# Relational graph convolution with its weight products in [3,2] by [2,3] blocks

## The chip, the cores and the metric

The kernel runs on one core of one Trainium2 chip. The metric is the device time of one execution in microseconds (us). A core has TensorE (PE; its weight loads are listed apart, as PEld), VectorE (DVE), ScalarE (ACT), GpSimd (POOL) and SyncE (SP), which issues most of the transfers. Each works through its own queue in order, and semaphores hold an instruction until what it needs is there. Everything is float32.

## What is computed

A graph of 384 nodes with 12,672 typed edges passes through an attention layer and then a relational graph network. The change is in the latter's two convolution layers:

```python
def _rgcn_conv(x, src, dst, edge_type, basis, comp, root, bias):
    n = x.shape[0]
    W = jnp.einsum('rb,bio->rio', comp, basis)
    h_all = jnp.einsum('ni,rio->rno', x, W)
    counts = jnp.zeros((R, n), x.dtype).at[edge_type, dst].add(1.0)
    norm = 1.0 / counts[edge_type, dst]
    msg = h_all[edge_type, src] * norm[:, None]
    agg = jax.ops.segment_sum(msg, dst, num_segments=n)
    return agg + x @ root + bias
...
x = jax.nn.relu(h_text @ w_in + b_in)
for l in range(L):
    h_in = x
    x = _rgcn_conv(x, src, dst, edge_type, basis[l], comp[l], root[l], conv_bias[l])
    x = jax.nn.relu(x)
    x = x + h_in
    x = _batchnorm(x, bn_gamma[l], bn_beta[l])
h_final = x @ w_out + b_out
```

Here R = 6 relations, four bases for each of L = 2 layers, and 768 features. The kernel never forms W. It computes H_b = x @ basis_b for the four bases, and for each basis a mixed adjacency matrix At_b, the sum over relations of comp[r, b] times the counts A_r, divided by the number of edges of relation r that end in each node. The aggregate is then the sum over b of At_b^T H_b, a product over 4 × 384 = 1,536 rows.

## The kernel before

The first part, up to about 371 us of the span, is the attention layer, the input projection (`ps_x`) and, beside them, the tables of edge counts: GpSimd scatters counts into a table in memory (`atab`), which is read back into `A` as six matrices of 384x384 (lines 850 to 854) and summed over sources by GpSimd (`add_up`, lines 355 and 356). This part is not changed but for the first weight loads.

Then, for each layer:

- **Bases.** Node features lie transposed: `XT` has six tiles of 128 features by 384 nodes. For each basis, H has three blocks of 128 nodes by 768 outputs. The first two node blocks, two halves of the input features and two halves of the outputs form a [2,2] by [2,2] block product that is done in seven products with sums (`node_sums`, `weight_sums`, `last_sums`, all on VectorE). The third node block is done plainly in four. That is 11 products of 3 matmuls, each 128x128 weights by 384 columns: 33 matmuls a basis. The 18 plain ones (line 985, the loop over `c`) come first and the sums are made beside them. The last product of a basis (`rest`) is done within the next one. Results go from PSUM to `H_` by copies on ScalarE (lines 991 to 1006) and additions on VectorE (992, 1000, 1002).
- **Divisors and mixes**, in layer 0, put between the products by the table `between`. `share(r)` (lines 358 to 369) sums A_r's counts over all partitions with a matmul by ones, turns zero counts into one on ScalarE (364, 365), takes a reciprocal on VectorE (366) and multiplies A_r by it (367). `mix` forms At from A: on ScalarE for r = 0 (346) and on VectorE for the other five relations, one instruction of 128x1152 for each of four bases (348). Layer 1 mixes A again with its own coefficients, beside its bases.
- **Root.** x @ root, transposed, in 36 matmuls of 384 columns (line 1019) that stay in six PSUM banks `pr`; the aggregate is partly added there.
- **Aggregate.** Seven products for each pair of output tiles (`ps_c`, line 1077) with the sums `T1` to `T4` of At and `feature_sums` of H on VectorE; then `take` adds to `XN`, `rectify`, `measure` and `normalise_layer` do ReLU, the residual and the batch normalisation of each feature tile. `XN` becomes the next layer's `XT`.

Weights come through `wpool`, five buffers of up to 8 KB a partition, in thirds of a basis. TensorE, VectorE, GpSimd, SyncE and (from the second projection on) ScalarE run in the order in which the program writes the instructions. PSUM has eight banks, handed out by `next_bank` in the order of last use.

Of the kernel before, what the change touches and what calls it, by code (L numbers as in the profile page):

```python
# [10 lines left out]
F32 = mybir.dt.float32  # L11
# [6 lines left out]
P = 128  # L18
N = 384
# [9 lines left out]
HC = DC // 2  # L29
# [15 lines left out]

BQ, BK, BV, BIQ, BIK, BIV, B_IN, CB, GAM, BET, NCOL = 0, 8, 16, 24, 32, 40, 48, 54, 66, 78, 90
# [5 lines left out]
def gnn_kernel(ctx: ExitStack, tc: tile.TileContext, out, x, edges, chunks, cols, rows, small,  # L52
               wq, wk, wv, wiq, wik, wiv, wo, w_in, basis, root, w_out):
# [297 lines left out]
    taken = []  # L351
# [5 lines left out]

    def share(r):

        ps = next_bank("ps_cnt", [i for i in range(8) if i not in taken])  # L360
        nc.tensor.matmul(ps[:, :N], ones, sums[r], start=True, stop=True)
        rn = late.tile([P, N], F32, tag="rn", name="rn", bufs=2)

        nc.scalar.activation(rn, ps[:, :N], AF.Relu, bias=minus)
        nc.scalar.activation(rn, rn, AF.Identity, bias=ones[:, 0:1])
        nc.vector.reciprocal(rn, rn)
        nc.vector.tensor_tensor(A[:, r], A[:, r], rn[:, None, :].to_broadcast([P, NT, N]), ALU.mult)
        if r + 4 < R:
            add_up(r + 4)


    with ExitStack() as inner:
# [358 lines left out]
        for g in range(STEPS + 1):  # L731
            f = g + LEAD
            if g < STEPS:
                turn_probs(g)
            if f < STEPS:
                exponents(f)
            if f - 1 in total:
                normalise(f - 1)
            if f + 1 < STEPS:
                scores(f + 1)  # L740
            if g == STEPS:
                ps_y = next_bank("ps_y", (0,))
                multiply_o(ps_y, 2, 0, range(KD - 1))
            if g > 0:
                gather(g - 1)
            if f + 2 == STEPS:

                w_x = [act_tile("w_x") for _ in range(2)]
                for half in range(2):
                    load_rows(w_x[half], w_in[half])  # L750
                w_first = [wload(basis[0, 0, part], (2, DC), "w_c") for part in range(3)]
                w_first += [wload(basis[0, 1, part], (2, DC), "w_c") for part in range(2)]
# [153 lines left out]
    with tc.tile_pool(name="conv", bufs=1) as cp:  # L906

        def block(X, n, i):

            return X.rearrange("p (c i) n -> p i c n", i=2)[:, i, :, n * P:(n + 1) * P]

        def node_sums(X):
            S = cp.tile([P, 4, 3, P], F32, tag="S", name="S")
            for i, a, b, op in ((0, block(X, 1, 0), block(X, 1, 1), ALU.add), (1, S[:, 0], block(X, 0, 0), ALU.subtract),
                                (2, block(X, 0, 0), block(X, 1, 0), ALU.subtract),
                                (3, block(X, 0, 1), S[:, 1], ALU.subtract)):
                nc.vector.tensor_tensor(S[:, i], a, b, op)  # L920
            return S

        def weight_sums(w):
            T13 = keep.tile([P, 3, 2, HC], F32, tag="hT", name="T13")
            T2 = keep.tile([P, 3, HC], F32, tag="mask8", name="T2")
            for c in range(3):
                nc.vector.tensor_tensor(T13[:, c], w[c][:, :, HC:], w[c][:, 0, :].rearrange("p (o d) -> p o d", o=2),
                                        ALU.subtract)
                nc.vector.tensor_tensor(T2[:, c], w[c][:, 1, HC:], T13[:, c, 0], ALU.subtract)
            return T13[:, :, 0], T2, T13[:, :, 1]  # L930

        def last_sums(w, T2):
            T4 = cp.tile([P, 3, HC], F32, tag="T4", name="T4")
            for c in range(3):
                nc.vector.tensor_tensor(T4[:, c], w[c][:, 1, :HC], T2[:, c], ALU.subtract)
            return T4

        w_first = [w_first[:3], w_first[3:]]

        def load_basis(l, b):  # L940
            w = w_first.pop(0) if w_first else []
            return w + [wload(basis[l, b, part], (2, DC), "w_c") for part in range(len(w), 3)]


        def shares(*rs):
            return lambda: [share(r) for r in rs]

        def mixes(l, r, *bs):
            return lambda: mix(l, r, At, bs)

        between = {(0, 2, 0): shares(0), (0, 2, 1): shares(1),
                   (0, 2, 2): shares(2), (0, 2, 4): lambda: [share(3), mix(0, 0, At)],
                   (0, 3, 0): shares(4), (0, 3, 1): shares(5),
                   (0, 3, 4): lambda: [mix(0, r, At) for r in range(1, R)],
                   (1, 0, 0): mixes(1, 0, 0, 1, 2, 3)}
        for i in range(10):
            between[1, (i + 1) // 3, (i + 1) % 3] = mixes(1, 1 + i // 2, *((0, 1), (2, 3))[i % 2])

        def go_between(*site):
            between.pop(site, lambda: None)()  # L960

        S = node_sums(XT)
        w = load_basis(0, 0)
        T = weight_sums(w)
        for l in range(L):

            H_ = cp.tile([P, B, NT, DC], F32, tag="H", name="H")
            rest = lambda: None
            for b in range(B):
                hs = [[H_[:, b, n, i * HC:(i + 1) * HC] for i in range(2)] for n in range(NT)]  # L970
                pe, pf, pb, pc, pa = [next_bank("ps_g", [i for i in range(8) if i not in taken[-1:]])[:, :N]
                                      for _ in range(5)]
                taken[:] = ring[-5:]
                kept = ring[-2:]

                def times(ps, x, y, start=False):

                    for c in range(3):
                        nc.tensor.matmul(ps, x[:, c], y(c), start=start and c == 0, stop=(c == 2),  # L979
                                         skip_group_check=not start)  # L980

                for c in range(3):
                    for ps, n, i, o, first in ((pa, 0, 0, 0, True), (pe, 2, 0, 0, True), (pf, 2, 0, 1, True),
                                               (pb, 0, 1, 0, True), (pe, 2, 1, 0, False), (pf, 2, 1, 1, False)):
                        nc.tensor.matmul(ps, block(XT, n, i)[:, c], w[c][:, i, o * HC:(o + 1) * HC],  # L985
                                         start=(first and c == 0), stop=(c == 2 and (i == 1 or ps is pa)))
                    if c == 0:
                        rest()
                        T4 = last_sums(w, T[1])
                    go_between(l, b, c)  # L990
                nc.scalar.copy(hs[0][0], pa)  # L991
                nc.vector.tensor_tensor(hs[0][0], hs[0][0], pb, ALU.add)
                times(pc, S[:, 0], lambda c: T[0][:, c], True)
                nc.scalar.copy(hs[2][0], pe)
                nc.scalar.copy(hs[2][1], pf)
                nc.scalar.copy(hs[1][1], pc)
                times(pa, S[:, 1], lambda c: T[1][:, c])
                nc.scalar.copy(hs[0][1], pa)
                times(pc, S[:, 3], lambda c: w[c][:, 1, HC:])
                nc.vector.tensor_tensor(hs[0][1], hs[0][1], pc, ALU.add)  # L1000
                times(pa, S[:, 2], lambda c: T[2][:, c])
                nc.vector.tensor_tensor(hs[1][1], hs[1][1], pa, ALU.add)

                def rest(pa=pa, X=XT, T4=T4, dst=hs[1][0]):
                    times(pa, block(X, 1, 1), lambda c: T4[:, c])
                    nc.scalar.copy(dst, pa)

                if b + 1 < B:
                    w = load_basis(l, b + 1)
                    T = weight_sums(w)  # L1010
                go_between(l, b, 4)


            w = [wload(root[l, part], (2, DC), "w_c") for part in range(3)]
            XN = xtp.tile([P, KC, N], F32, tag="XT", name="XN")
            pr = [next_bank("ps_c", [i for i in range(8) if i not in kept])[:, :N] for _ in range(KC)]
            for k in range(KC):
                for o in range(KC):
                    nc.tensor.matmul(pr[o], w[k // 2][:, k % 2, o * P:(o + 1) * P], XT[:, k, :], start=(k == 0),  # L1019
                                     stop=(k == KC - 1))  # L1020
                if k == 0:
                    rest()
                go_between(l, B, k)
# [97 lines left out]
            for o in range(KC):  # L1121
                begin(o)
# [147 lines left out]
```

## Time and profile before

| What | Value |
|---|---|
| time, median of three runs | 715.99 us (715.95 to 715.99) |
| the profiled execution | 717.47 us, of which its span 715.7 |
| granted TensorE clock | 0.995 of full |
| layer 0: bases and root | about 370.9 to 483.9 us of the span |
| layer 0: aggregate | to about 527 |
| layer 1: bases and root | about 527.7 to 636.3 |
| layer 1: aggregate | to 677.3 |
| output projection and its normalisation | to the end |

A matmul in float32 leaves two records of a matmul and two of a weight load. A record's own duration (486 ns for 384 columns) is longer than its share of time, since records overlap: the pace is found by dividing a run of records in the chain by their number. In a line of groups the columns are: line, engine, operation, output and inputs, shapes, count, then busy time and mean duration, then the idle time before and what ended it.

### The profile page before, as it was taken

To read this page: it belongs to the slowest core of one execution; us is meant where nothing else is said; L and a number is where in the kernel's file an instruction comes from. 1 tells how busy PE (TensorE), PEld (TensorE's weight loads), DVE (VectorE), ACT (ScalarE), POOL (GpSimd) and SP (SyncE) were. 2 spreads that over 40 slices of the span, in tenths; PEclk is the share of its full clock that TensorE was granted. 3 is DMA by queue.
4 is the path that set the end of the run, shared out by engine and by line. 5 is a ranking of instruction groups with operands and counts; after the bars stand their busy time and mean duration, and the time that the engine had idled before them with its cause. 6 is when DMAs were issued, how large, how long until landed. Compare 5 with 4: busy or idle time off the path is not lost.

```text
span 715.7 us, 9149 instructions
## 1 busy us (share of the span) xinstructions
PE 699.9 (98%) x3228; PEld 527.9 (74%) x3228; DVE 512.6 (72%) x1307; ACT 157.6 (22%) x360; POOL 308.1 (43%) x239
## 2 busy tenths in 40 slices
PE   8999999999999999999999999999999999999995
PEld 7759999999997444478985555558975555579943
DVE  5886697868886699787534279798878766507756
ACT  3211111111111577410221124202131111011100
POOL 1366777778687788687786542000000000120000
PEclk9999999999999999999999999999999999999999
DMA  8788787373562622733424994311104322700001
GB/s 303 267 279 264 228 250 212 80 243 67 203 209 43 177 2 1 221 44 45 89 0 103 250 288 153 133 44 45 45 0 133 102 69 94 308 1 1 1 30 59
DMA packets 69180, 91.04 MB, mean 127 GB/s; under 512 B 22940, under 2 KB 50688, under 8 KB 68750
## 3 DMA queue, kind: packets, MB, share of 16 engines
q1 hardware_dynamic: 46830, 78.45, 32.6%
q0 software_dynamic: 21296, 9.60, 10.8%
q10 hardware_dynamic: 1008, 2.41, 0.9%
q8 instruction: 25, 0.41, 0.2%
q14 instruction: 21, 0.17, 0.1%
HBM read 79.27 MB, written 11.16 MB: 126 GB/s over the span
## 4 chain that ended last, share of the span: by engine, by line
PE 87%; DVE 10%; ACT 2%; DMA 1%; issue 0%; DVEq 0%; ACTq 0%
PE ps_g L985 12%; PE ps_g L979 10%; PE ps_k L402 10%; PE ps_c L1077 10%; PE ps_v L402 8%; PE ps_q L420 6%; PE ps_q L402 5%; PE ps_f L1183 4%; DVE At L348 4%; PE ps_y L402 3%; PE ps_c L1019 3%; PE ps_x L402 3%; PE ps_o L707 2%; PE ps_s L662 2%; PE ps_pT L696 2%; PE ps_v L586 2%
## 5 line engine op out<-in xcount | busy, mean ns | idle before, releaser
L283 POOL DMA_INDIRECT atab<-count,at x99 | 166.3, 1679 | 44.2 <-issue 23.5
L278 POOL DMA_INDIRECT mtab<-m_val,at x99 | 103.4, 1045 | 57.6 <-issue 22.9
L1170 POOL TENSOR_TENSOR x_sb<-x_sb,room 128x1024 f32<-128x1024 f32 x3 | 7.0, 2348 | 188.9 <-DMA room<-in_rows 188.9
L348 DVE SCALAR_TENSOR_TENSOR At<-A,small_sb,At 128x1152 f32<-128x1152 f32 x40 | 53.6, 1414 | 0.0
L979 PE MATMUL ps_g<-T,S 128*128 128x384 f32 x144 | 49.1, 486 | 0.0
L985 PE MATMUL ps_g<-w_c,XN 128*128 128x384 f32 x144 | 47.7, 487 | 1.1 <-DVE XN L1107 1.1
L985 PE MATMUL ps_g<-w_c,XT 128*128 128x384 f32 x144 | 47.9, 486 | 0.0
L420 PE MATMUL ps_q<-hT,w_q 128*128 128x384 f32 (+1 forms) x160 | 43.4, 435 | 1.4 <-DVE hT L108 1.4
L985 PEld LDWEIGHTS ps_g<-w_c,XN 128*128 128x128 f32 x144 | 27.3, 190 | 20.2 <-DVE XN L1107 1.4
L979 PEld LDWEIGHTS ps_g<-T,S 128*128 128x128 f32 x144 | 27.3, 190 | 19.2 <-ACT H L991 0.4
L985 PEld LDWEIGHTS ps_g<-w_c,XT 128*128 128x128 f32 x144 | 27.3, 190 | 18.8
L420 PEld LDWEIGHTS ps_q<-hT,w_q 128*128 128x128 f32 x160 | 30.1, 200 | 14.1 <-ACT hT L101 1.7
L1077 PE MATMUL ps_c<-At,H 128*128 128x192 f32 x216 | 36.4, 326 | 0.0
L1077 PEld LDWEIGHTS ps_c<-At,H 128*128 128x128 f32 x216 | 35.4, 190 | 0.5
L402 PE MATMUL ps_k<-T,S 128*128 128x192 f32 x192 | 35.1, 326 | 0.0
L1107 DVE TENSOR_TENSOR XN<-XN,ps_c 128x192 f32<-128x192 f32 x38 | 12.5, 349 | 30.8 <-ACT XN L1063 19.7
L402 PEld LDWEIGHTS ps_k<-T,S 128*128 128x128 f32 x192 | 31.8, 190 | 0.0
L1183 PE MATMUL ps_f<-w_out,XN 128*128 128x512 f32 (+1 forms) x84 | 31.1, 531 | 0.0
L675 DVE CUSTOM_DVE_ANT_0 s<-ps_s,mask 128x384 f32<-128x384 f32 x48 | 24.5, 550 | 5.3 <-PE ps_s L662 5.3
L267 DVE SCALAR_TENSOR_TENSOR same<-cells,own,later 128x128 f32<-128x128 int32 x99 | 28.0, 350 | 0.4
L267 DVE SCALAR_TENSOR_TENSOR same<-keys,key,weigh 128x128 f32<-128x128 int32 x99 | 27.9, 349 | 0.0
L1183 PEld LDWEIGHTS ps_f<-w_out,XN 128*128 128x128 f32 x84 | 15.9, 190 | 14.9 <-issue 14.3
(298 smaller groups left out, 1411.6 us busy)
## 6 DMA issues: line engine op xcount, KB each, us to landing
w_c<-in_basis SPq DMA_DIRECT2D x96, 192.0 KB, 4.1
atab<-zero SPq DMA_DIRECT2D x36, 192.0 KB, 5.2
A<-atab POOLq DMA_DIRECT2D x12, 576.0 KB, 9.0
keys<-keys_d SPq DMA_DIRECT2D x25, 192.0 KB, 5.1
w_c<-in_root SPq DMA_DIRECT2D x6, 768.0 KB, 7.1
w_q<-in_wiq SPq DMA_DIRECT2D x16, 256.0 KB, 6.4
w_k<-in_wk SPq DMA_DIRECT2D x16, 256.0 KB, 5.8
w_k<-in_wik SPq DMA_DIRECT2D x16, 256.0 KB, 3.0
```

Source lines behind the costliest of these rows:

```text
L267: nc.vector.scalar_tensor_tensor(same, row[:, n, :], mine[:, c:c + 1], times, ALU.is_equal, ALU.mult, accum_out=count[:, i, c:c + 1])
L278: nc.gpsimd.indirect_dma_start(mtab[c // PER][:, :], bass.IndirectOffsetOnAxis(at[:, 0, c:c + 1], 0), m_val[:, c:c + 1], None)
L283: nc.gpsimd.indirect_dma_start(atab[0 if i < 11 else i % 2][:, :], bass.IndirectOffsetOnAxis(at[:, 1, c:c + 1], 0), count[:, 1, c:c + 1], ...
L348: nc.vector.scalar_tensor_tensor(At[:, b], A[:, r], w, At[:, b], ALU.mult, ALU.add)
L402: nc.tensor.matmul(ps, a[:, k, :], b[:, k, :], start=start and k == 0, stop=(k == 3), skip_group_check=not start)
L420: nc.tensor.matmul(ps[o][:, c], wt_[:, k, o * P:(o + 1) * P], src[:, k, c], start=(k == 0 and c.start == 0), stop=(k == KD - 1 and c.stop ...
L675: nc.vector.tensor_tensor_reduce(s[j], ps[:, :N], mask8[:, t, :], -scale, 3.0e38, ALU.add, ALU.min, tops[:, j:j + 1])
L979: nc.tensor.matmul(ps, x[:, c], y(c), start=start and c == 0, stop=(c == 2), skip_group_check=not start)
L985: nc.tensor.matmul(ps, block(XT, n, i)[:, c], w[c][:, i, o * HC:(o + 1) * HC], start=(first and c == 0), stop=(c == 2 and (i == 1 or ps is ...
L1019: nc.tensor.matmul(pr[o], w[k // 2][:, k % 2, o * P:(o + 1) * P], XT[:, k, :], start=(k == 0), stop=(k == KC - 1))
L1077: nc.tensor.matmul(ps, x[:, c], y[:, c], start=start and c == 0, stop=stop and c == 5, skip_group_check=True)
L1183: nc.tensor.matmul(p, XT[:, k, t * P:(t + 1) * P], w[k // 2][:, k % 2, c0:c1], start=(k == 0), stop=(k == KC - 1))
```

## The change

Each basis is now a [3,2] by [2,3] block product: three blocks of 128 nodes, two halves of the inputs (three tiles each), three thirds of 256 outputs. It has 15 products (a plain one has 18) from 11 sums of node blocks (`X_SUMS`, per layer) and 10 sums of weight blocks (`W_SUMS`, per basis). The second layer's root is a fifth such block in which weights and features change places in the matmul, so that the result is transposed and goes straight to `XN`; the first layer's root stays as it was. A product adds to one of four chains, each in a PSUM bank, and the bank is read between products, so that its running sum serves several blocks of H.

`POOLED` gives the weight sums that GpSimd makes: five in layer 0's last basis, seven and then five a block in layer 1. T3 and T4 go to GpSimd too. The divisors of two relations share a pair of matmuls with 64 output partitions each, two activations, one reciprocal, and four copies on ScalarE that spread each half over 128 partitions. The three pairs come after steps 30, 39 and 49 of the 60 in layer 0; the mixes are spread over single steps from 36 to 75 (from 60 on within the root) and, in layer 1, over steps 1 to 55. The conv bias of layer 1 moves into `rectify`, and the aggregate of layer 1 begins in banks of its own.

```diff
-HC = DC // 2
+HC2 = DC // 3
...
+X_SUMS = (
+    (6, 1, 2, -1, 4),
+    (7, -1, 5, -1, 6),
+    (8, 1, 1, 1, 3),
...
+W_SUMS = (
+    (6, 1, 2, 1, 5),
+    (7, 1, 1, 1, 6),
+    (8, 1, 4, 1, 7),
+    (9, 1, 0, -1, 6),
+    (10, 1, 1, 1, 2),
+    (11, 1, 3, 1, 9),
+    (12, 1, 4, 1, 11),
+    (13, 1, 0, -1, 2),
+    (14, 1, 12, -1, 13),
+    (15, -1, 1, -1, 12),
+)
+PRODUCTS = (
+    (2, 1, 0, ((4, 1),)),
+    (6, 6, 1, ((7, 1), (8, -1))),
+    (7, 7, 0, ((7, 1),)),
+    (5, 8, 2, ((7, 1),)),
+    (9, 9, 1, ((6, -1),)),
+    (10, 10, 0, ((8, -1),)),
+    (3, 4, 3, ((4, 1),)),
+    (11, 5, 0, ((5, -1),)),
+    (12, 12, 3, ((3, -1),)),
+    (13, 13, 0, ((2, 1),)),
+    (8, 11, 3, ((0, 1), (6, -1))),
+    (14, 0, 1, ((0, 1), (2, 1))),
+    (15, 14, 0, ((0, 1), (3, -1))),
+    (0, 15, 3, ((1, -1),)),
+    (16, 3, 0, ((6, -1),)),
+)
...
+    def count_shares(r, among):
+
+        ps = next_bank("ps_cnt", among)
+        for j in range(2):
+            nc.tensor.matmul(ps[j * HD:(j + 1) * HD, :N], ones[:, :HD], sums[r + j], start=True, stop=True)
+        both = late.tile([P, N], F32, tag="both", name="both")
+        nc.scalar.activation(both, ps[:, :N], AF.Relu, bias=minus)
+        nc.scalar.activation(both, both, AF.Identity, bias=ones[:, 0:1])
+        nc.vector.reciprocal(both, both)
+        for j in range(2):
+            shared[r + j] = late.tile([P, N], F32, tag="rn", name="rn", bufs=2)
+            for half in range(2):
+                nc.scalar.copy(shared[r + j][half * HD:(half + 1) * HD, :], both[j * HD:(j + 1) * HD, :])
+            if r + j + 4 < R:
+                add_up(r + j + 4)
...
     def share(r):
...
+        nc.vector.tensor_tensor(A[:, r], A[:, r], shared.pop(r)[:, None, :].to_broadcast([P, NT, N]), ALU.mult)
...
+        ON_DVE, ON_POOL = (-2, -1, 0, 1, 2, 4, 5, 6, 9, 10), (-4, -3, -1, 0, 2, 3, 5, 6, 8, 9)
+        SOONER = (-8, -7, -6, -2, -5, -1, 0, 1, 2, 3)
+        POOLED = {3: range(4, 9), 5: (0, 1, 2, 3, 4, 7, 8), **{g: (1, 2, 4, 7, 8) for g in range(6, 10)}}
...
+        put(0, 30, lambda: count_shares(0, free_banks()))
+        put(0, 39, lambda: count_shares(2, free_banks()))
+        put(0, 49, lambda: count_shares(4, free_banks()))
+        for r, step in zip(range(R), (34, 36, 47, 48, 58, 59)):
+            put(0, step, share, r)
+        for b in range(B):
+            put(0, (36, 37, 38, 40)[b], lambda b=b: mix(0, 0, At, (b,)))
+        for i, step in enumerate((41, 43, 44, 46, 51, 52, 54, 55, 57, 60, 61, 63, 64, 66, 67, 69, 70, 72, 73, 75)):
+            put(0, step, lambda i=i: mix(0, 1 + i // B, At, (i % B,)))
+        for b in range(B):
+            put(1, 1 + 2 * b, lambda b=b: mix(1, 0, At, (b,)))
+        for i in range((R - 1) * B):
+            put(1, 8 + 2.5 * i, lambda i=i: mix(1, 1 + i // B, At, (i % B,)))
...
+                begin_with(step + 3)
+                if g != 5 * l or k > 2 or l:
+                    sum_weights_at(g, k)
+                if g + 1 < end:
+                    for ahead in range(-8, 0):
+                        if k == NPROD + ahead:
+                            sum_weights_at(g + 1, ahead)
+                x, w, c, targets = PRODUCTS[k]
...
+                if g < root:
+                    for j in range(3):
+                        nc.tensor.matmul(ps, x[:, j], w[:, j], start=start and j == 0, stop=(j == 2),
+                                         skip_group_check=not start)
+                else:
+                    for o in range(2):
+                        for j in range(3):
+                            nc.tensor.matmul(ps[:, o * P:(o + 1) * P], w[:, j, o * P:(o + 1) * P], x[:, j],
+                                             start=start and j == 0 and o == 0, stop=(j == 2), skip_group_check=True)
+                for to, sign in targets:
...
+                    if (g, to) not in begun:
+                        begun.add((g, to))
+                        if sign > 0:
+                            nc.scalar.copy(dst, src)
+                        else:
+                            nc.scalar.activation(dst, src, AF.Identity, scale=-1.0)
+                    else:
+                        nc.vector.tensor_tensor(dst, dst, src, ALU.add if sign > 0 else ALU.subtract)
...
+                for f in between.pop((l, step), ()):
+                    f()
...
+            T4 = mroom
...
-            nc.vector.tensor_tensor(T3, q(1, 1), q(0, 1), ALU.subtract)
-            nc.vector.tensor_tensor(T4, q(1, 0), T2, ALU.subtract)
+            nc.gpsimd.tensor_tensor(T3, q(1, 1), q(0, 1), ALU.subtract)
+            nc.gpsimd.tensor_tensor(T4, q(1, 0), T2, ALU.subtract)
```

A line of `PRODUCTS` names the feature block or sum, the weight block or sum, the chain, and the blocks of H with the sign with which the chain's bank is added to each. A number from 6 on is a sum. A line of `W_SUMS` is its number and two signed inputs. `ON_DVE`, `ON_POOL` and `SOONER` (for the third basis of layer 0) give the step in a block at which each sum is issued; a negative one lies in the block before. `begin_with` issues the feature sums that are needed up to three steps ahead, and `sum_weights_at` the weight sums of this step.

## The prediction

> **What bounds the kernel now.** I read the page first (part 1, busy time), then the windows of the two convolution layers, then the chain of waits, then the groups of VectorE and GpSimd.
>
> ```profile
> PE 699.9 (98%) x3228; PEld 527.9 (74%) x3228; DVE 512.6 (72%) x1307; ACT 157.6 (22%) x360; POOL 308.1 (43%) x239
> ```
>
> TensorE has 16 us of idle time in 715.7. So time is won only by giving TensorE fewer columns, and lost wherever it begins to wait. The windows (after the stretch and its length: PE, PEld, DVE, ACT, POOL, with counts) show who has room:
>
> ```profile
> 411.00:437.00 26.00, 26.00 (x82) 15.27 (x81) 20.90 (x22) 7.58 (x15) 13.51 (x13) 1.00 1.03 267
> 437.00:459.00 22.00, 21.34 (x67) 12.31 (x66) 16.64 (x16) 9.39 (x14) 0.00 (x0) 1.00 0.23 83
> 459.00:483.00 24.00, 24.00 (x76) 14.16 (x75) 24.00 (x19) 0.48 (x1) 0.00 (x0) 1.00 0.30 100
> 549.00:570.00 21.00, 21.00 (x66) 12.35 (x65) 15.08 (x18) 2.87 (x6) 0.00 (x0) 1.00 0.33 108
> ```
>
> VectorE is the second engine: 15 of 21 us in a block of layer 1 and full from 459 to 483, beside layer 0's root.
>
> ```profile
> 332.45 3.45 PE ps_y L840 x16
> 335.91 1.75 PE ps_h L176 x16
> ...
> 390.24 3.87 PE ps_g L985 x12
> ...
> 435.44 0.59 ACT rn L364
> 436.05 0.62 ACT rn L365
> 436.67 4.58 ACT At L346 x4
> 441.25 0.48 ACT H L1006
> 441.87 0.88 PE ps_cnt L361 x2
> ...
> 459.46 26.58 DVE At L348 x20
> ...
> 526.87 0.80 DVE XN L1107 x3
> 527.71 11.88 PE ps_g L985 x36
> ```
>
> The chain gives TensorE's pace (a float32 matmul leaves two records): 3.87/12 = 0.3225 us a record at 384 columns, 3.45/16 = 0.216 at 256, 1.75/16 = 0.109 at 128. It also shows what is fragile: at 436 to 442 ScalarE takes its queue in order (count, weights, then the copy of a product) and TensorE waits for that copy.
>
> ```profile
> L366 DVE RECIPROCAL rn<-rn 128x384 f32<-128x384 f32 x4 | 10.2, 2545 | 0.0
> L348 DVE SCALAR_TENSOR_TENSOR At<-A,small_sb,At 128x1152 f32<-128x1152 f32 x40 | 53.6, 1414 | 0.0
> L927 DVE TENSOR_TENSOR T<-w_c 128x768 f32<-128x768 f32 x15 | 14.3, 952 | 0.0
> L355 POOL TENSOR_TENSOR sum<-A 128x384 f32<-128x384 f32 x6 | 6.8, 1129 | 13.2 <-DMA A<-atab 13.2
> L1170 POOL TENSOR_TENSOR x_sb<-x_sb,room 128x1024 f32<-128x1024 f32 x3 | 7.0, 2348 | 188.9 <-DMA room<-in_rows 188.9
> ```
>
> **What the Trainium skill says.** "SBUF — State Buffer", Who interferes with whom: a VectorE instruction with two SBUF inputs and a GpSimd instruction that reads SBUF exclude each other, whole instruction for whole instruction. The trace has only the direction in which VectorE came first: a GpSimd sum of 0.99 us took 1.20 at 433.09, where VectorE's product A×rn ran until 433.44. No GpSimd sum here has a two-input VectorE instruction start within it, but for 0.1 us at its end. "TensorE: Matmul & The Clock Gate", Why this matters for your kernels: matmuls with few output partitions, put on different PSUM partitions, run concurrently. The trace agrees: four records of ps_o (64 partitions, 384 columns) take 0.80 us in the chain, not 4 × 0.3225.
>
> **The change, part by part.** "Step" is one of the 15 products of a block; steps count from 0 in each layer.
>
> Bases. A block loses 66 records of 384 columns, 66 × 0.3225 = 21.3, and gets 15 products × 6 records of 256, 90 × 0.216 = 19.4: −1.85 each, eight blocks −14.8.
>
> Second root. 72 × 0.3225 = 23.2 becomes 15 × 12 records of 128 columns, 180 × 0.109 = 19.6: −3.6. PEld runs beside PE at 190 ns a record and is full at 192 columns (35.4 us for 216), so a bound by weight loads at 0.1625 a record is the other end: 29.3, +6.1. I take 0.109, since the rows of L176 load a new 128x128 block each record at that pace.
>
> Counts. Six single counts of 0.65 are 3.9; three pairs at 0.80 are 2.4: −1.5. TensorE's waits at 441 (0.66) and at 492 to 495 (1.1, VectorE late with the node sums) should go, as VectorE starts layer 0's mixes earlier: −1.8.
>
> TensorE's gain so far: −21.7.
>
> VectorE and ScalarE now have, per block, ten weight sums of 128x768 (0.95 alone, 0.87 in a row; about 1.8 on GpSimd, between 0.99 for 384 and 2.35 for 1024), ten additions from PSUM of 256 (0.42, the x_sb addition from PSUM of that size) and nine copies (0.4). Before: nine weight sums of mixed size, 5.8 us, and three additions, 1.65. In layer 1 with its six mixes (1.33 in a row) VectorE has 4.4 + 4.2 + 8.0 = 16.6 of 19.4 us, and GpSimd 9. It fits on average; what counts is order. Chains share a PSUM bank: step 7 must wait for the reading of 5, 8 for 6, 10 for 8, 13 for 10, 14 for 12, 4 for 1. There is one product, 1.3 us, between most of them.
>
> (a) Layer 0's first block: six sums are queued before step 3, later ones every step. Following the queue, step 7 waits 0.5 and step 8 0.6: +1.1.
>
> (b) Divisors. Each pair now puts on ScalarE: two activations (1.2), then four 64x384 copies (1.7) that wait for the reciprocal (2.55). All copies of later products stand behind them. From the end of step 30: count done 0.8, activations 2.1, reciprocal 4.7, copies 6.4, step 31's two copies 7.2. Step 34 needs the latter and could start at 4.7: +2.5. Pair two (step 39) is alike: reciprocal done 4.3 after its step, ScalarE free 6.1, step 40's copy 6.5; step 43 could start 4.7 after: about +2.5; step 44 then waits for the additions of 42, queued behind a mix: +1.7. Pair three (step 49): VectorE, behind two shares of 1.3 and a mix, ends the reciprocal about 5.5 after the step, and step 52 waits for the subtraction of 50 behind it: +2.6; step 48 waits +0.6 for a sum. Together +10. If the queues stand better, 3; if shares and mixes collide more, 14. Halving the reciprocals (−7.6 on VectorE) is what keeps the 20 mixes done before the root ends (traced: 73.5 us after step 30, needed at 81), so it is worth nothing more.
> GpSimd's count sums before pair one end at 411.6 (trace, r = 1); step 30 ends about 412, so I cost no wait there.
>
> (c) Between layers. Before, the first 36 records use plain weights and node blocks, and sums are made under them. Now step 1 needs a feature sum, which VectorE makes only after the last tile is normalised: it ends 4.5 us after TensorE's last product (526.9 to 531.4), plus 0.56 for the sum. Step 0 covers 1.3 of 5.2: 3.9 idle for 0.8 before, +3.1. Nothing else is in TensorE's queue there.
>
> (d) Mixes in layer 1 lie at steps 0, 3, 5, 8, 10, 13. The subtraction of 5 stands behind two sums and the mix of 3: step 7 waits 0.2; the addition of 6 stands behind a mix: step 8 waits 0.45. Three blocks × 0.65, and 0.3 in the first: +2.3.
>
> Hidden: T3 and T4 go to GpSimd (2.6 each, by the same two rows), needed 13 us after the root; T1, T2 and four feature sums (6.1) lie under four products of 1.95 (7.8), which no longer wait for the root's banks. Weight loads are as many bytes and are asked for at least 7 us ahead (7 to 9 landed before in the full windows).
>
> Sum: −21.7 + 1.1 + 10 + 3.1 + 2.3 = −5.2. The profiled span 715.7 becomes 710.5 (its run lasted 717.5, so that one 712.3); the median, 715.99, becomes 710.8: I say 711.
>
> **Rivals.** R1, queues stand better: (b) costs 3 and (d) nothing, 711 − 9 = 702. For it: ScalarE is only 22% busy. Against it: it is order and not share that delays, as at 441.
> R2, slower: GpSimd's sums hold VectorE. If the exclusion holds with GpSimd first, a block of layer 1 needs 9.0 (GpSimd) + 4.4 + 8.0 = 21.4 us in turn, and up to 25.6 with the additions behind them, against 19.4. I work out 3 more per block for three, 1.5 in the first, 0.5 in the root, 4 in layer 0's last: +15, 726; half held, 718. It decides from 0.26 us per sum (6.6 us over 25 sums in the blocks and root). For it: the skill and 433.09. Against it: VectorE's sum at 435.26, begun in the last 0.1 us of a GpSimd sum, was not longer. I name 722 as its time.
> R3: the root's weight loads bind at 0.1625: 711 + 9.7 = 721. Against it: L176.
>
> **Numbers.** Forecast 0.50 (its own range 706 to 716: 0.43 faster, 0.04 same, 0.03 slower); R1 0.20, faster; R2 0.25 (0.20 slower, 0.05 same); R3 0.05, slower. Differences under 0.2% (1.4 us) can't be told from none. Faster 0.63, same 0.09, slower 0.28. The range 702 to 722 takes in R1 and R2's middle, and leaves out some 0.2.
>
> **What would show it.** Right: records of 0.216 and 0.109 in the chain; TensorE idle of 2 to 3 us behind ScalarE's copies of the divisors, three times; about 4 us behind the first feature sum of layer 1. Wrong: VectorE's sums longer than 0.95 while GpSimd adds (R2), the root near 29 us (R3), no idle at the divisors (R1). A late transfer, costed at nothing, would show as TensorE waiting for conv_w.

## The result: 758.0 us, 6% slower

| | before | after |
|---|---|---|
| time, median | 715.99 us (715.95 to 716.67) | 758.02 us (756.8 to 765.57) |
| span of the profiled execution | 715.7 | 755.0 |
| ratio | | 1.0607, 95% interval 1.0538 to 1.0676 |
| granted clock, mean over the span | 0.995 | 0.973 |

Ratios, here and below, are to the kernel before, run beside the other, and use fast runs alone.

The first line of the page of the kernel after shows the main fact. TensorE is busy for 699.7 us, as before (699.9), though it has 19.9 us of columns less to do (14.8, 3.6 and 1.5). Its idle time has grown from 15.8 us to 55.3:

```profile
PE 699.7 (93%) x3528; PEld 575.5 (76%) x3528; DVE 577.9 (77%) x1369; ACT 164.8 (22%) x393; POOL 399.0 (53%) x275
```

Cutting the span where TensorE starts each kind of product gives the stages (us; a product of the old bases that is done within the root is counted with the bases):

| Stage | before | after | difference | predicted |
|---|---|---|---|---|
| layer 0, bases and root | 113.1 | 127.5 | +14.4 | +1.5 |
| layer 0, aggregate | 43.8 | 45.3 | +1.5 | −1.1 |
| layer 1, bases | 85.2 | 104.5 | +19.3 | −2.0 |
| layer 1, root | 23.2 | 20.1 | −3.1 | −3.6 |
| layer 1, aggregate | 41.0 | 49.7 | +8.7 | 0 |

The column "predicted" sorts the prediction's own terms: for layer 0's first row −7.4 of columns, −1.5 of counts, −0.7 of waits, +1.1 of (a) and +10 of (b); for layer 1's bases −7.4, +3.1 and +2.3.

The windows of the kernel after over these stages of layer 1 (stretch, its length, then PE, PEld, DVE, ACT, POOL with counts, the granted clock, the share of the transfers and GB/s):

```profile
542.10:646.60 104.50, 87.39 (x362) 70.90 (x362) 88.21 (x102) 18.44 (x42) 38.12 (x18) 0.93 0.26 86
646.60:666.70 20.10, 20.10 (x182) 20.10 (x181) 8.41 (x14) 3.32 (x9) 9.17 (x5) 1.00 0.30 107
666.70:716.40 49.70, 43.38 (x255) 43.08 (x254) 40.83 (x79) 4.08 (x10) 16.16 (x5) 0.93 0.10 32
```

Two losses are to be seen in the first line. TensorE idles for 17.1 us. And it is busy for 87.4 us with 360 records that take 77.8 at the pace of 0.216: the clock, 0.93 in the mean, is at half for 13.7 us of the stage, which is 6.8 of these 9.6 us. The root alone runs without either. From the first product of layer 0 to the end of layer 1's aggregate the clock is at half for 37.5 us, a loss of 18.8; in the kernel before it is never at half there.

What TensorE waited for in the kernel after (product, what released it; us in total, times, longest):

```profile
PE ps_g L1098 <- DVE H L1119: 17.8, 12, 4.0
PE ps_c L1186 <- DVE XN L1216: 8.7, 2, 6.3
PE ps_cnt L410 <- POOL sum L404: 6.5, 1, 6.5
PE ps_g L1098 <- DVE x_room L982: 4.1, 1, 4.1
PE ps_g L1098 <- POOL room L982: 4.0, 4, 1.3
```

Of these 41.1 us, 30.6 end on VectorE and 10.5 on GpSimd. The groups of VectorE and GpSimd in the kernel after say why it is late; the mixes took 1,414 ns before, and a sum of this shape 952:

```profile
L396 DVE SCALAR_TENSOR_TENSOR At<-A,small_sb,At 128x1152 f32<-128x1152 f32 x40 | 67.1, 1704 | 0.0
L982 DVE TENSOR_TENSOR room<-w_c,room 128x768 f32<-128x768 f32 x27 | 35.5, 1323 | 0.3
...
L1287 POOL TENSOR_TENSOR x_sb<-x_sb,room 128x1024 f32<-128x1024 f32 x3 | 9.1, 3054 | 0.0
...
L1194 POOL TENSOR_TENSOR At<-At 128x1152 f32<-128x1152 f32 x2 | 7.6, 3792 | 37.3 <-DVE x_room L1191 37.3
```

The timeline of a block of layer 1 (start, duration; the last bracket is the idle time before, and what ended it):

```profile
593.22 1.41 DVE L396 SCALAR_TENSOR_TENSOR At<-A,small_sb,At 128x1152 f32<-128x1152 f32 x1
593.52 5.66 POOL L982 TENSOR_TENSOR room<-w_c,room 128x768 f32<-128x768 f32 x2 [10.46 <-PE ps_g L1098]
...
594.88 2.64 DVE L396 SCALAR_TENSOR_TENSOR At<-A,small_sb,At 128x1152 f32<-128x1152 f32 x1
...
597.44 2.55 DVE L982 TENSOR_TENSOR room<-w_c,room 128x768 f32<-128x768 f32 x1
599.23 1.56 PE L1098 MATMUL ps_g<-room,XN 128*128 128x256 f32 x6 [1.25 <-POOL room L982]
```

The mix at 593.22 began before the GpSimd sum and kept its 1.41 us; the next mix, begun while GpSimd adds, took 2.64, and the sum behind it 2.55 for 0.95. GpSimd pays too: 5.66 for two sums that alone take 1.81 each. That is rival R2. The additions to H behind these (line 1119) then come late, and they are what frees the PSUM chain for the next product.

### The profile page after: what moved, and what is told of

Its sections match the earlier page's. It is cut to its first block, busy times and chain, and to the rows that moved or that the text cites. A ratio compares the mean times of both kernels' runs of the same rounds, so it can differ in the third digit from the quotient of the medians.

```text
span 755.0 us, 9992 instructions
## 1 busy us (share of the span) xinstructions
PE 699.7 (93%) x3528; PEld 575.5 (76%) x3528; DVE 577.9 (77%) x1369; ACT 164.8 (22%) x393; POOL 399.0 (53%) x275
## 5 line engine op out<-in xcount | busy, mean ns | idle before, releaser
L1098 PE MATMUL ps_g<-room,x_room 128*128 128x256 f32 x354 | 87.8, 398 | 7.4 <-DVE x_room L982 4.1
L1098 PEld LDWEIGHTS ps_g<-room,x_room 128*128 128x128 f32 x354 | 69.7, 200 | 23.0 <-DVE H L1119 6.1
L396 DVE SCALAR_TENSOR_TENSOR At<-A,small_sb,At 128x1152 f32<-128x1152 f32 x40 | 67.1, 1704 | 0.0
L982 POOL TENSOR_TENSOR room<-w_c 128x768 f32<-128x768 f32 x13 | 25.5, 1964 | 72.5 <-PE ps_c L1186 28.8
L982 POOL TENSOR_TENSOR room<-w_c,room 128x768 f32<-128x768 f32 x12 | 30.5, 2540 | 41.7 <-PE ps_g L1098 33.2
L1098 PE MATMUL ps_g<-w_c,x_room 128*128 128x256 f32 x144 | 38.8, 409 | 12.0 <-DVE H L1119 12.0
L1119 DVE TENSOR_TENSOR H<-H,ps_g 128x256 f32<-128x256 f32 x80 | 31.3, 415 | 16.0 <-PE ps_g L1098 9.0
L1098 PEld LDWEIGHTS ps_g<-w_c,x_room 128*128 128x128 f32 x144 | 28.1, 201 | 18.9 <-DVE H L1119 14.8
L1117 ACT ACTIVATE H<-ps_g 128x256 f32<-128x256 f32 x40 | 15.4, 385 | 96.6 <-PE ps_g L1098 96.6
L982 DVE TENSOR_TENSOR room<-w_c,room 128x768 f32<-128x768 f32 x27 | 35.5, 1323 | 0.3
```

Source lines behind the costliest of these rows:

```text
L396: nc.vector.scalar_tensor_tensor(At[:, b], A[:, r], w, At[:, b], ALU.mult, ALU.add)
L982: engine.tensor_tensor(dst, a, b, ALU.add if sb > 0 else ALU.subtract)
L1098: nc.tensor.matmul(ps, x[:, j], w[:, j], start=start and j == 0, stop=(j == 2), skip_group_check=not start)
L1119: nc.vector.tensor_tensor(dst, dst, src, ALU.add if sign > 0 else ALU.subtract)
```

## Experiments

Theory 1 in the first three experiments is that the two engines' two-input work excludes each other (R2), theory 2 that VectorE simply has too much to do, so that work given back to it makes it worse.

**All of GpSimd's new work on VectorE, or a part of it.** The first edit, with both parts (in the expectations this kernel is called e1):

```diff
-        POOLED = {3: range(4, 9), 5: (0, 1, 2, 3, 4, 7, 8), **{g: (1, 2, 4, 7, 8) for g in range(6, 10)}}
+        POOLED = {}
...
-            nc.gpsimd.tensor_tensor(T3, q(1, 1), q(0, 1), ALU.subtract)
-            nc.gpsimd.tensor_tensor(T4, q(1, 0), T2, ALU.subtract)
+            nc.vector.tensor_tensor(T3, q(1, 1), q(0, 1), ALU.subtract)
+            nc.vector.tensor_tensor(T4, q(1, 0), T2, ALU.subtract)
```

The second kernel has the first part alone, the third the second alone.

> All weight sums, T3 and T4 on VectorE, nothing else changed. Theory 1 (a GpSimd sum and a two-input VectorE instruction exclude each other): every VectorE sum and mix is back at 0.95 and 1.41 us, a block of layer 1 is set by VectorE's own 21 us (10 sums 8.7, 10 additions 4.2, 6 mixes 8) in place of 25.3, layer 1's aggregate takes 41 to 42 us in place of 49.7: about 758 - 4x4 - 8 - some 3 in layer 0 = 731 us. Theory 2 (VectorE has too much work and GpSimd relieves it): 24 us of sums come on top of a full VectorE, 765 to 780 us.

> Only the weight sums go back to VectorE; T3 and T4 stay on GpSimd. Theory 1: blocks of layer 1 as in the first kernel (21 us), the aggregate of layer 1 stays near 49 us with feature sums of 3 us: about 739 us. Theory 2: 765 us or more.

> Only T3 and T4 go back to VectorE; the weight sums stay on GpSimd. Theory 1: blocks stay at 25 us, the four feature sums that open each aggregate fall from 3.3 to 0.95 us, so layer 1's aggregate loses its 6.3 us wait and the slow clock behind it: about 749 us. Theory 2: two subtractions of 1.3 us come before the feature sums on VectorE: 758 us or 3 more.

Measured: 746.2 us (ratio 1.0378, 95% interval 1.0307 to 1.0449), 744.3 (1.0374, 1.0327 to 1.0421) and 760.4 (1.0619, 1.0566 to 1.0671). The sums brought about a third of the loss back (13.7 of 42.0 us), so work put back on the busier engine made it faster: theory 2 falls as the only cause. Layer 1's bases went from 104.5 to 93.3. But the numbers of theory 1 were missed too, and T3 and T4 gave nothing. The timeline of the first of these kernels says why: with T3 and T4 gone from GpSimd, the next work in its queue moved up to the same place.

```profile
662.25 9.20 POOL L1287 TENSOR_TENSOR x_sb<-x_sb,room 128x1024 f32<-128x1024 f32 x3 [226.57 <-DMA room<-in_rows]
662.27 0.95 DVE L1206 TENSOR_TENSOR x_room<-H 128x768 f32<-128x768 f32 x1
663.25 2.99 DVE L1206 TENSOR_TENSOR room<-x_room,H 128x768 f32<-128x768 f32 x1
...
666.17 3.09 DVE L1206 TENSOR_TENSOR H<-H 128x768 f32<-128x768 f32 x1
669.18 3.09 DVE L1206 TENSOR_TENSOR x_room<-H,room 128x768 f32<-128x768 f32 x1
...
672.60 4.21 PE L1186 MATMUL ps_c<-x_room,room 128*128 128x192 f32 x12 [6.15 <-DVE XN L1216]
```

The three additions to `x_sb` are in the kernel before too (2.35 us each, no feature sum beside them). Here the feature sums take turns with them, TensorE waits 6.15 us, and its next 12 records take 4.21 us instead of 2.1.

**The exclusion by itself.** The kernel before, with scratch work on GpSimd: twenty additions of two halves of a weight tile whose results nobody reads, placed behind each third of a basis of layer 1.

```diff
...
+                for i in range(1 + (c < 2)):
+                    nc.gpsimd.tensor_tensor(scratch, w[:, 0, :], w[:, 1, :], ALU.add)
...
```

> The kernel before, with five GpSimd additions of 128x768 from a weight tile to a scratch tile beside each of layer 1's four bases; nobody waits for them but the weight buffers. Theory 1: VectorE's mixes and weight sums that meet one last up to 1.8 us longer each; mean of the mixes in layer 1 well above 1.41 us, and TensorE begins to wait: 718 to 730 us. Theory 2: durations unchanged, 716 us.

Measured: 730.2 us in both of its two runs (1.0195, 1.0175 to 1.0215). As a control, GpSimd was given work of one column and then a write that reads nothing, at the same places:

```diff
...
+                    nc.gpsimd.tensor_tensor(scratch[:, :1], w[:, 0, :1], w[:, 1, :1], ALU.add)
+                    nc.gpsimd.memset(scratch, 0.0)
...
```

> The kernel before with scratch work on GpSimd in layer 1's bases, at the places of the twenty additions of the run before, but of another kind: an addition of one column and a write of a constant over 128x2048, which reads nothing. If two-input work on both engines is what excludes, the writes cost VectorE nothing: 716 to 717, VectorE's two-input sums of two tiles there at their former 0.55 us. If any GpSimd access to SBUF holds VectorE: as with the additions, near 730, the sums near 1 us.

Measured: a ratio of 1.0003 (0.9975 to 1.0032). The kernel before, run beside it, took 718 to 740 us itself, so the ratio counts here and not the time; the last two kernels below were run beside it too. Groups in layer 1's bases (527 to 640): of the kernel before, then with the additions, then with the writes:

```profile
L929 DVE TENSOR_TENSOR T<-w_c,T 128x384 f32<-128x384 f32 x12 | 6.7, 558 | 0.4
```

```profile
L929 DVE TENSOR_TENSOR T<-w_c,T 128x384 f32<-128x384 f32 x12 | 14.1, 1178 | 0.4
...
L967 POOL TENSOR_TENSOR scratch<-w_c 128x768 f32<-128x768 f32 x12 | 25.5, 2124 | 55.0 <-DMA w_c<-in_basis 54.4
```

```profile
L929 DVE TENSOR_TENSOR T<-w_c,T 128x384 f32<-128x384 f32 x12 | 6.7, 559 | 0.4
...
L968 POOL MEMSET scratch<- 128x2048 f32 x11 | 19.9, 1805 | 0.7
```

With additions beside it the sum of 558 ns takes 1,178, with writes 559. In layer 1 this cost nothing, as VectorE has room there (bases 85.5 us for 85.2). The time was lost where VectorE is full: the first weights of layer 1 land while layer 0's mixes run, and with them the first five pieces of scratch work. The mixes of layer 0 (458 to 528), again with additions and with writes:

```profile
L348 DVE SCALAR_TENSOR_TENSOR At<-A,small_sb,At 128x1152 f32<-128x1152 f32 x20 | 34.4, 1795 | 0.0
```

```profile
L348 DVE SCALAR_TENSOR_TENSOR At<-A,small_sb,At 128x1152 f32<-128x1152 f32 x20 | 26.7, 1409 | 0.0
```

TensorE then waited 5.85 us at 488.27 for the last mix and 3.43 at 501.45 for a feature sum. So it is two-input work on VectorE against reading work on GpSimd, as the Trainium skill has it ("SBUF — State Buffer", Who interferes with whom). The timeline of the kernel with additions shows the turns: in layer 1 VectorE's sum of 0.56 us becomes 2.05 when it has to let one GpSimd addition pass.

```profile
561.59 0.95 DVE L927 TENSOR_TENSOR T<-w_c 128x768 f32<-128x768 f32 x1
561.84 2.37 POOL L967 TENSOR_TENSOR scratch<-w_c 128x768 f32<-128x768 f32 x1 [34.07 <-DMA w_c<-in_basis]
562.58 2.05 DVE L929 TENSOR_TENSOR T<-w_c,T 128x384 f32<-128x384 f32 x1
```

**None of the new work on GpSimd, nor the additions to `x_sb`.** The first kernel of above, with the three additions on VectorE as well (e5 in the expectations):

```diff
-            nc.gpsimd.tensor_tensor(x_sb[:, t, :], x_sb[:, t, :], rowsB[:, 2, :], ALU.add)
+            nc.vector.tensor_tensor(x_sb[:, t, :], x_sb[:, t, :], rowsB[:, 2, :], ALU.add)
```

> e1 with the three additions of the bias row to x_sb moved from GpSimd to VectorE as well, so that no GpSimd instruction reads SBUF beside VectorE after the counts. Exclusion: the feature sums that open layer 1's aggregate last 0.95 us in place of 3.0, TensorE's wait of 6.2 us there and the half clock behind it go: 8 us less than e1, about 737 us. If it was VectorE's own order (four T sums, four feature sums), the wait stays: 745 us.

Measured: 735.9 us (1.029, 1.0247 to 1.0332), as expected. The aggregate of layer 1 is back at 41.0 us. The opening of it, in the timeline of this kernel, beside the one above:

```profile
660.04 0.96 DVE L1206 TENSOR_TENSOR room<-x_room,H 128x768 f32<-128x768 f32 x1
660.92 0.95 DVE L1206 TENSOR_TENSOR H<-H 128x768 f32<-128x768 f32 x1
661.12 2.11 PE L1186 MATMUL ps_c<-x_room,x_room 128*128 128x192 f32 x12
661.79 0.95 DVE L1206 TENSOR_TENSOR x_room<-H,room 128x768 f32<-128x768 f32 x1
```

What GpSimd's part costs is thus 22.1 us (758.0 − 735.9) of the 42.0 by which the change made it slower; by stages 11.2 in layer 1's bases, 8.7 in its aggregate, and 2.8 in layer 0, where executions of one order differ by as much. This is a net figure: the edit also loads VectorE with all the sums, so the exclusion alone costs more. And some of it is left. GpSimd's old count sums, which no edit touches, now meet VectorE's new weight sums in layer 0: here one of them takes 2.74 us and the next 1.74 where 0.95 is usual, and TensorE waits 2.13.

```profile
404.86 2.74 DVE L986 SCALAR_TENSOR_TENSOR room<-w_c,room 128x768 f32<-128x768 f32 x1
405.24 1.53 POOL L403 TENSOR_TENSOR sum<-A 128x384 f32<-128x384 f32 x1
...
409.65 1.87 PE L1098 MATMUL ps_g<-room,XT 128*128 128x256 f32 x6 [2.13 <-DVE H L1119]
```

The other 19.9 us are to be found in this kernel.

**The rest in layer 1: VectorE's queue.** The same kernel, with layer 1's mixes spread further, so that the last of them lie beside the root:

```diff
-            put(1, 8 + 2.5 * i, lambda i=i: mix(1, 1 + i // B, At, (i % B,)))
+            put(1, 5 + 3.3 * i, lambda i=i: mix(1, 1 + i // B, At, (i % B,)))
```

> e5 with layer 1's twenty VectorE mixes spaced by 3.3 steps in place of 2.5, so that they reach into its root. If VectorE's load sets the blocks of layer 1 (21 us of work for 19.4 of TensorE), blocks fall from 22 to about 20 us and the bases of layer 1 from 93 to 85 us: about 729 us. If it is the queue order at steps 5 to 8 alone, no more than 2 us less than e5.

Measured: 729.0 us (1.0169, 1.0131 to 1.0207). The windows of layer 1's bases, without the spread and with it:

```profile
539.90:633.20 93.30, 83.06 (x362) 68.99 (x361) 82.36 (x119) 18.44 (x42) 0.00 (x0) 0.96 0.30 96
537.90:625.80 87.90, 81.18 (x362) 69.00 (x361) 78.12 (x117) 18.43 (x42) 0.00 (x0) 0.98 0.32 102
```

The bases take 87.9 us instead of 93.3 (85 were expected), the root 21.0 instead of 20.1. The total of 729 is as expected, but in part by luck: the spread gained 4.5 us, and of the rest 3.1 lie in the bases and root of layer 0, which it does not touch. So part of what was left in layer 1 was VectorE's load. By the prediction's figures it has 16.6 us a block with five sums on GpSimd; with all ten it has 16.6 + 5 × 0.95 = 21.4, over TensorE's 19.4. The change is caught between the two: VectorE can neither keep these sums nor share them.

**The rest in layer 0: the divisors.** Two edits to the kernel without GpSimd's part: the pairs of divisors and what hangs on them five steps later; and single divisors, each with its own reciprocal, at steps 30, 33, 41, 45, 52 and 56. Of the first edit, without the products by the divisors and the mixes, which move along:

```diff
-        put(0, 30, lambda: count_shares(0, free_banks()))
-        put(0, 39, lambda: count_shares(2, free_banks()))
-        put(0, 49, lambda: count_shares(4, free_banks()))
+        put(0, 35, lambda: count_shares(0, free_banks()))
+        put(0, 44, lambda: count_shares(2, free_banks()))
+        put(0, 54, lambda: count_shares(4, free_banks()))
...
```

> e5 with the three pairs of divisors, the shares and the mixes of layer 0 five steps (6.5 us) later. If TensorE's wait for the first pair is only for tables that come late, its 4.9 us and the half clock behind it (2 us) go, and the rest of the block pattern stays: 6 to 7 us less than e5, about 730 us. If the wait is made elsewhere again (the mixes then end late and hold layer 0's aggregate), 735 to 740 us.

> e5 with one reciprocal and one full count matmul for each relation, as in the kernel before, and none of the four ScalarE copies, at steps 30, 33, 41, 45, 52, 56. If the prediction's step (b) holds (ScalarE's queue behind the reciprocal of a pair), the waits of about 3 and 4 us in layer 0's last two blocks shrink by half though VectorE has 7.6 us more: 3 to 6 us less than e5, about 733 us. If VectorE's load is what holds them, 3 to 7 us more.

Measured: 731.1 us (1.0223, 1.0182 to 1.0263) for the later pairs. The gain can't be put down to the move: bases and root of layer 0 took 123.0 us, while two executions of the unmoved order in two kernels took 124.7 and 121.6. The single divisors gave 747.0 (1.0425, 1.0398 to 1.0452), above both expectations: bases and root of layer 0 grew to 137.7. Three more reciprocals, 7.6 us of VectorE, came with 11 us more; TensorE waited up to 5.5 us for additions behind them. But 4.7 us of waiting were for the second count sum: the table's transfers were issued at 395.4 us in this execution and at 386.4 in the one it is compared with. So this run speaks against single divisors here, but how much they cost is not shown.

The later pairs and the spread mixes together:

> All sums, T3, T4 and the residual additions on VectorE, the divisor pairs five steps later in layer 0, and the mixes of layer 1 spread into the root. The two moves touch different layers, so if VectorE's load and the late divisors are what is left, their gains add: 735.9 less 4.8 (the later divisors alone) less 6.9 (the spread alone) = 724.2, range 721 to 728. If each of them only moved the same wait on, no gain beside the better one: 729. Below 716 only if TensorE no longer waits in the bases, which neither theory expects: VectorE's sums and additions in a block of layer 1 without the mixes are about 17 us of 19.4.

Measured: a ratio of 1.0186 (1.0093 to 1.028). The interval holds the ratios of both theories (724.2/716 = 1.0115 and 729/716 = 1.018), so the median doesn't decide. By stages layer 1's gain is there (bases 87.9, root 21.0); layer 0's can't be told (122.9, again between the 124.7 and 121.6 of the unmoved order).

**The paired divisors in the kernel before**, at the places of its old table (`count_shares` and `share` as in the change):

```diff
...
-        between = {(0, 2, 0): shares(0), (0, 2, 1): shares(1),
-                   (0, 2, 2): shares(2), (0, 2, 4): lambda: [share(3), mix(0, 0, At)],
-                   (0, 3, 0): shares(4), (0, 3, 1): shares(5),
+        between = {(0, 2, 0): lambda: pair(0), (0, 2, 2): shares(0, 1),
+                   (0, 2, 4): lambda: [pair(2), mix(0, 0, At)],
+                   (0, 3, 0): lambda: [shares(2, 3)(), pair(4)], (0, 3, 2): shares(4, 5),
...
```

> The kernel before with the divisors of two relations in one reciprocal, as in the change, at the places of the old table (pairs behind the first, second and third run of products of the third basis and the start of the fourth), nothing else. It saves three reciprocals on VectorE (about 2.5 us each), which before did not hold TensorE: 714 to 717, no change. If ScalarE's four copies a pair hold the copies of H behind them, as the prediction had it, 718 to 726.

Measured: a ratio of 1.0137 (1.0078 to 1.0195): slower, as the prediction's step (b) would have it. The stages of the profiled execution say how much of it is the divisors: bases and root of layer 0 took 121.4 us instead of 113.1. The other 13.7 us by which this execution is longer lie ahead of the bases, in a part that the edit leaves alone. Of the timeline of this kernel:

```profile
455.00 2.09 ACT L371 COPY rn<-both 64x384 f32<-64x384 f32 x4 [5.31 <-DVE both L367]
456.22 2.62 DVE L376 TENSOR_TENSOR A<-A,rn 128x1152 f32<-128x1152 f32 x2
457.11 4.69 ACT L346 ACTIVATE At<-A,small_sb 128x1152 f32<-128x1152 f32 x4
461.70 0.46 ACT L1016 COPY H<-ps_g 128x384 f32<-128x384 f32 x1
462.31 1.55 PE L363 MATMUL ps_cnt<-sum,ones 128*64 128x384 f32 x4 [7.98 <-ACT H L1016]
```

ScalarE waits for the reciprocal, makes its four copies and four mixes, and only then comes the copy of a product that frees TensorE's bank: 7.98 us of wait. The same queue order cost 0.66 us in the kernel before; the pairing lengthens it.

None of these versions beats the kernel before.

## Why the prediction was wrong

It said 711 us, faster with 0.63, and the range ended at 722; the time was 758. The cause of more than half of the loss was on the list, as R2 with a chance of 0.25, but at 722 to 726.

**The step that failed: "VectorE has 4.4 + 4.2 + 8.0 = 16.6 of 19.4 us, and GpSimd 9. It fits on average".** The forecast set the two engines' work side by side, and its sum has no term for their exclusion. In the trace they take turns: the period of a block is 25.3 us (a weight sum at 592.35, the same of the next block at 617.64), against 19.4 of TensorE. R2 had this mechanism and mis-sized it, with "3 more per block"; it is 5.9, and in the same paragraph stood the figures for it: 21.4 us a block in turn, up to 25.6 with the additions behind them. (Its threshold of 0.26 us a sum counts 25 sums; `POOLED` has 27 there.) The one argument against R2, a sum begun in the last 0.1 us of a GpSimd sum, could not show a wait longer than 0.1 us, so it was no evidence.

**The exclusion was not followed to all of GpSimd's work.** "Hidden: T3 and T4 go to GpSimd" was costed at nothing because their results are needed late. But what they hold up is VectorE's feature sums, needed at once, and behind them stand the `x_sb` additions, which the change does not touch. Measured: 8.7 us in layer 1's aggregate, all of it back when these ran on VectorE. For GpSimd's part as a whole, +15 was R2's figure, and 22.1 us came back net.

**Step (b), +10, was right in its waits.** Without GpSimd's part, the trace has waits of 2.65 (predicted 2.5, step 34, behind ScalarE), 2.88 and 0.66 (predicted 2.5 and 1.7, pair two) and 2.35 (predicted 2.6, pair three): 8.5 us in all. The 0.6 at step 48 did not come. In the kernel after the first of them is hidden under a wait of 6.5 for the second count sum, which "I cost no wait there" put at nothing: the table's transfers were issued at 391.4 us and not at 386.4 as before. In the other kernels with the change they were issued between 386.3 and 395.4.

**The price of a wait was wrong.** Each was costed at its own length. The wait of 2.88 us in the kernel without GpSimd's part ended at 440.49. Windows of 3.41 us around it (the third column from the end is the clock):

```profile
438.07:441.48 3.41, 0.99 (x5) 0.88 (x6) 1.46 (x4) 3.12 (x5) 0.00 (x0) 1.00 0.00 0
441.48:444.90 3.42, 2.76 (x7) 1.77 (x6) 3.42 (x5) 0.38 (x1) 0.00 (x0) 0.50 0.00 0
444.90:448.31 3.41, 3.41 (x9) 2.69 (x9) 3.41 (x5) 0.00 (x0) 0.00 (x0) 0.50 0.37 95
448.31:451.72 3.41, 3.41 (x17) 2.99 (x17) 3.41 (x5) 1.03 (x3) 0.00 (x0) 1.00 0.38 141
```

So 6.8 us at half clock follow a wait of 2.9: a loss of 3.4 us more. With clocks of 0.89 and 0.91 over 410 to 440 and 440 to 480, layer 0 of this kernel loses 30 × 0.11 + 40 × 0.09 = 6.9 us in this way; in the kernel before both are 1.00. That is most of what its 124.7 us have over the predicted 114.6.

**Step (d), +2.3, can't be judged apart.** Its order of additions behind mixes holds with five sums on GpSimd and no exclusion, and no run has both.

**Right:** the columns (90 records at 0.216 and, in the root, 20.1 us for 180 records, predicted 19.6), which refutes R3; step (c), 4.08 us idle behind the first feature sum, predicted 3.9; and no wait for `conv_w` is in the list. Step (a), +1.1, came as one wait of 0.67. The waits of 0.34 and 0.78 in layer 0's aggregate went as predicted, but a new one of 2.37 behind VectorE (at 532.51) and the half clock after it took more. The 19.9 us of columns are really saved, and more than that is lost in two ways: as idle time, and as half clock after it.

**Open:** no run changes a wait alone to try what halves the clock; the rule below is read off the traces. How layer 0's +14.4 divides between a late table and the clock differs from execution to execution.

## What to carry to other kernels

Before moving two-input work from VectorE to GpSimd to relieve it, add the two engines' times in turn, not side by side, and look at everything else that GpSimd will then do at a new time. Where TensorE is nearly full, trading its columns for sums on a second engine that is 70% busy pays only where the sums fit without waits: here it did in the root alone (−3.1 us). Work that GpSimd had before counts too, once VectorE has new sums beside it. Price a wait of TensorE at its length and at the clock that may follow: here 1.7 us for each 3.41 at half clock.

## What the runs showed of the hardware

- In these traces half clock goes by how busy TensorE is within a step of 3.41 us (by the records' modelled ends), not by the length of a gap. In each trace with more than one change of the clock the changes lie whole multiples of 3.41 us apart: up to the end of layer 1's aggregate a stretch at half clock lasts 3.41, 6.83 or 10.24 us. Where the steps begin differs from trace to trace. The numbers that follow are of all 13 traces, cut at these steps, from 365 to 700 us. A step at full clock in which TensorE was busy for 0.41 of the time or less was followed by half clock, 47 times of 47. From 0.43 on none was, and between lies one of each kind (0.418 not, 0.426 yes). A step at half clock was followed by full clock where TensorE was busy for 0.87 or more, and by half clock again where it was for 0.82 or less. So a gap of 2.87 us in the kernel after cost no clock: it ended at 442.44, and the end of a step at 441.55 divides it.

```profile
438.13:441.55 3.42, 1.43 (x7) 0.93 (x5) 1.30 (x1) 2.04 (x4) 0.00 (x0) 1.00 0.11 41
441.55:444.96 3.41, 1.56 (x6) 1.06 (x6) 3.00 (x7) 2.01 (x3) 0.00 (x0) 1.00 0.00 0
444.96:448.37 3.41, 3.28 (x15) 2.92 (x16) 3.41 (x6) 0.37 (x1) 0.00 (x0) 1.00 0.08 29
```

The gap of 2.88 us shown further above lies within one step, which leaves TensorE 0.99 us of 3.41, and cost two steps. The Trainium skill ("TensorE: Matmul & The Clock Gate", Why this matters for your kernels) warns of gaps of more than about 3 us; here gaps of 2.13 and 2.65 us were each followed by a step at half clock too. The wait of 6.5 us in the kernel after shows the slow return: half clock begins at 414.24 within the wait, and ends only when a step has been filled.

```profile
410.83:414.24 3.41, 1.09 (x4) 0.19 (x2) 1.34 (x3) 0.37 (x1) 0.08 (x1) 1.00 1.03 389
414.24:417.65 3.41, 0.00 (x0) 0.00 (x0) 0.00 (x0) 0.00 (x0) 3.33 (x4) 0.50 1.04 297
417.65:421.07 3.42, 2.66 (x5) 1.30 (x6) 0.00 (x0) 1.05 (x2) 3.09 (x4) 0.50 1.11 260
421.07:424.48 3.41, 3.41 (x10) 2.70 (x9) 3.23 (x2) 0.78 (x3) 2.92 (x3) 0.50 1.03 187
424.48:427.89 3.41, 3.05 (x15) 2.37 (x14) 2.64 (x4) 2.07 (x5) 1.57 (x2) 1.00 1.07 277
```

- The exclusion is paid whatever the size: in the control a GpSimd addition of one column took 1.18 us instead of 0.19 while a mix ran. GpSimd's writes of 1.80 us lay beside the same mixes and lengthened neither.
